# A triangle update and a gated pair layer: reordering the opening of the first stage

## The chip, the cores and the metric

The kernel runs on one core of a Trainium2 chip. The metric is the device time of one execution in microseconds; the time given for a kernel is the median of several executions. One further execution is taken with the hardware profiler, and the profile and the trace in this text come from it.

## The reference, cut to what matters

The input x is a 384 x 384 x 128 array in float32. Two layers follow each other. All matrices are 128 x 128.

```python
def _L0_conv_ref(z, ...):
    z_n = _layernorm(z, norm_g, norm_b)
    a = _linear(z_n, Wa, ba) * sigmoid(_linear(z_n, Wga, bga))
    b = _linear(z_n, Wb, bb) * sigmoid(_linear(z_n, Wgb, bgb))
    x = einsum('bijd,bjkd->bikd', a, b)
    x = _layernorm(x, normo_g, normo_b)
    return z + _linear(x, Wo, bo) * sigmoid(_linear(z_n, Wgo, bgo))

def _L1_conv_ref(pair, ...):
    left = pair @ W_left + b_left + (pair @ W_eq + b_eq)
    right_sum = sum(pair @ W_right + b_right, axis=2, keepdims=True)
    gate = sigmoid(pair @ W_gate + b_gate)
    out = (left * right_sum * gate) @ W_out + b_out
    return _layer_norm(out + pair, ln_scale, ln_bias)
```

Layer 0 needs, for every pixel, five products of the normalised x: the two factors a and b with their gates, and the output gate.

## The kernel before, in words

There are three stages. Stage 1 computes a, b and the output gate and writes them to arrays A, B and G in device memory, together with Z, which is x plus a bias. Stage 2 forms the 128 products over j, one for each channel, and the sums for the second norm. Stage 3 does the output product, the gate and all of layer 1. The change concerns only the beginning of stage 1.

Stage 1 works on tiles of x of 128 rows by 16 columns by 128 channels (1 MB). There are 72 tiles, each is done in four steps (TS) of four columns (CT), so there are 288 steps, numbered s; n is the tile and t the quarter. The schedule is manual: each engine executes its instructions in the order in which the program text emits them. An instruction that waits therefore holds up everything behind it on its engine or queue. The engines are PE (TensorE, the products), DVE (VectorE), ACT (ScalarE), POOL (GpSimd) and SP (SyncE, which issues most transfers).

One column of x goes through these helpers:

- `statistics` (DVE): bn_stats and bn_aggr give its mean and variance.
- `norm_factors` (POOL): four small operations make the reciprocal deviation `rstd` (with a power operation) and the offset `off`, for four to sixteen columns at a time.
- `normalise` (ACT): one instruction for each column writes the normalised column `zn`.
- `turn` (PE) transposes four columns into PSUM (`ptr`), and `turned_out` (ACT) copies them to SBUF as `zT`.
- `step` then forms, on PE in this order, `pga`, `pa`, `pgb`, the transposes of the next step, `pb`, and four small products `pgo`. ACT takes the sigmoids `sga` and `sgb`; DVE multiplies into `at` and `bt` and adds the gate's bias into `gs`. The sigmoid of `gs` (`gate`) is taken by ACT during the next step.
- `residual` (POOL): x plus b_out for a whole tile (`zb`), and the transfer to Z that follows it. POOL's queue also issues the transfers to A (after the tile's last `at`) and to G (after its last `gate`).

All products of stage 1 and the weights' preparation take their PSUM from one pool of six buffers (`pk`), which are used in turn: a product can start when the buffer six places earlier has been read. Four buffers hold x tiles, so the fetch of tile n+3 (at the first step of tile n) waits until tile n-1 has been read by all, its residual included.

Before step 0, `prepare` turns each weight: PE transposes it, DVE copies it (`raw`) and scales it by the norm's vector (`scaled`), and PE multiplies it with the norm's bias to give a correction of the weight's bias, which DVE adds. The transfers on SP stand in the order: four quarters of x's first tile, the norm's two vectors, the four biases, x's second tile, and so on. ACT's queue issues the five weights. `prepare` of ga and of a stand ahead of all statistics on DVE.

In the first four steps, DVE computes the statistics of four columns of tile 1 and of four columns of tile 2 in each step; from step 4 on, of four columns two tiles ahead. After step 4 the output weights are prepared: `ob_w`, `prepare("o")`, `center` (the identity less 1/128), the product `pc` of the two, and the sums and scalings of the weights and biases for layer 1. The residuals of tiles 0, 1 and 2 are computed in steps 4, 5 and 6, those of tile 3 and later each at the second step of the tile before.

Of the kernel before, what the change touches and what calls it, by code (L numbers as in the profile page):

```python
# [8 lines left out]
FP = mybir.dt.float32  # L9
AF = mybir.ActivationFunctionType  # L10
ALU = mybir.AluOpType
# [8 lines left out]
def kernel(ctx: ExitStack, tc: tile.TileContext, ins, out: bass.AP):  # L20
# [15 lines left out]
    nc = tc.nc  # L36
    ctx.enter_context(tc.manual_schedule())
    P = 128
    x = ins["x"][0]
    N, C = x.shape[1], x.shape[2]  # L40
# [46 lines left out]

    CG, CX, CT, BR = 64, 16, 4, 32  # L90
    TS = CX // CT
    NT = NB * (N // CX)
    with tc.tile_pool(name="wprep", bufs=6) as wp, tc.tile_pool(name="p1x", bufs=4) as px, tc.tile_pool(name="p1s", bufs=3) as ps, tc.tile_pool(
# [7 lines left out]
            rb, c = divmod(n, N // CX)  # L101
            return rb * P, c * CX

        def fetch(n, parts=1):
            if n >= NT:
                return
            r0, c0 = place(n)
            xt = px.tile([P, CX, C], FP, tag="xt", name=f"xt_{n}")
            for k in range(0, CX, CX // parts):
                nc.sync.dma_start(  # L110
                    out=xt[:, k : k + CX // parts, :], in_=x[r0 : r0 + P, c0 + k : c0 + k + CX // parts, :]
                )
            tiles[n] = {
                "x": xt,
                "st": ps.tile([P, CX, 6], FP, tag="st", name=f"st_{n}"),
                "mv": ps.tile([P, CX, 2], FP, tag="mv", name=f"mv_{n}"),
                "rstd": ps.tile([P, CX], FP, tag="rstd", name=f"rstd_{n}"),
                "off": ps.tile([P, CX], FP, tag="off", name=f"off_{n}"),
            }

        def statistics(n, t):
            if n >= NT:
                return
            for c in range(t * CT, (t + 1) * CT):
                nc.vector.bn_stats(tiles[n]["st"][:, c, :], tiles[n]["x"][:, c, :])  # L125
                nc.vector.bn_aggr(tiles[n]["mv"][:, c, :], tiles[n]["st"][:, c, :])

# [11 lines left out]
        def normalise(n, t, cs=range(CT)):  # L139
            if n >= NT:  # L140
                return
            g = tiles[n]
            for c in (t * CT + k for k in cs):
                nc.scalar.activation(  # L144
                    g["zn"][:, c, :], g["x"][:, c, :], AF.Identity,
                    bias=g["off"][:, c : c + 1], scale=g["rstd"][:, c : c + 1],
                )
# [25 lines left out]
        def gate(s):  # L173
# [4 lines left out]
            if t == TS - 1:  # L178
                r0, c0 = place(n)
                nc.gpsimd.dma_start(out=G[r0 : r0 + P, c0 : c0 + CX, :], in_=gt)  # L180
                tiles.pop(n - 1, None)

        def step(s):
            n, t = divmod(s, TS)
            r0, c0 = place(n)
            if t == 0:
                fetch(n + 3)
                if n:
                    norm_factors(n + 1)
                tiles[n]["at"] = po.tile([P, CX, P], FP, tag="at", name=f"at_{n}")  # L190
                tiles[n]["gt"] = po.tile([P, CX, C], FP, tag="gt", name=f"gt_{n}")
                if c0 % CG == 0:
                    bts[n // (CG // CX)] = po.tile([P, P, CG], FP, tag="bt", name=f"bt_{n}")
            at, bt = tiles[n]["at"], bts[n // (CG // CX)]
            k0 = c0 % CG + t * CT
            zT = turned.pop(s)
            ahead = (n + 1, t - 1) if t else (n, TS - 1)

            def proj(k):
                pk = ppp.tile([P, CT, P], FP, tag="pk", name=f"p{k}_{s}")  # L200
                nc.tensor.matmul(pk, lhsT=wT[k], rhs=zT, start=True, stop=True)  # L201
                return pk

            def sigmoid(k, pg):
                sg = ps.tile([P, CT, P], FP, tag="sg", name=f"sg{k}_{s}")
                nc.scalar.activation(sg, pg, AF.Sigmoid, bias=bcol["g" + k])  # L206
                return sg

            if n == 0:
                statistics(1, t)  # L210
                norm_factors(1, t * CT, t * CT + CT)
            statistics(n + 2, t)
            pga, pa = proj("ga"), proj("a")
            sga = sigmoid("a", pga)
            if s:
                gate(s - 1)
            normalise(*ahead, range(CT // 2))
            nc.vector.scalar_tensor_tensor(  # L218
                at[:, t * CT : (t + 1) * CT, :], pa, bcol["a"], sga, ALU.add, ALU.mult
            )  # L220
            if t == TS - 1:
                nc.gpsimd.dma_start(out=A[:, c0 : c0 + CX, r0 : r0 + P], in_=at)  # L222
            pgb = proj("gb")
            sgb = sigmoid("b", pgb)
            turn(s + 1)
            turned_out(s + 1)
            normalise(*ahead, range(CT // 2, CT))
            pb = proj("b")
            nc.vector.scalar_tensor_tensor(  # L229
                bt[:, :, k0 : k0 + CT].rearrange("d r c -> d c r"), pb, bcol["b"], sgb, ALU.add, ALU.mult  # L230
            )
            pgo = ppp.tile([P, CT, C], FP, tag="pk", name=f"pgo_{s}")
            for c in range(CT):
                nc.tensor.matmul(pgo[:, c, :], lhsT=zT[:, c, :], rhs=wT["go"], start=True, stop=True)  # L234
            gs = ps.tile([P, CT, C], FP, tag="gs", name=f"gs_{s}")
            nc.vector.tensor_tensor(gs, pgo, over(gate_bias, CT), ALU.add)
            gated[s] = gs
            if n == 1 and t < 3:
                residual(t)
            if n > 1 and t == 1:  # L240
                residual(n + 1)
            if k0 + CT == CG:
                b_out_of.extend((bt, r0, c0 + CX - CG, k) for k in range(0, P, BR))
            if t == TS - 1:
                store_b(len(b_out_of) if n == NT - 1 else 1)
# [11 lines left out]
        def prepare(k):  # L257
            both = ppp.tile([P, CT, P], FP, tag="pk", name="w_" + k)
            pt, pb = both[:, 0, :], both[:, 1, :]
            nc.tensor.transpose(pt, wT[k], ident)  # L260
            raw = wp.tile([P, P], FP, tag="raw", name="raw_" + k, bufs=2)
            nc.vector.tensor_copy(raw, pt)
            scaled = ctile([P, P], "wT_" + k)
            nc.vector.tensor_scalar(scaled, raw, og if k == "o" else ng, None, ALU.mult)
            if k in ("go", "o"):
                bias = o_bias if k == "o" else gate_bias
                nc.tensor.matmul(pb, lhsT=ob_w if k == "o" else nb_w, rhs=raw, start=True, stop=True)
                nc.vector.tensor_tensor(bias, pb, bias, ALU.add)
            else:
                nc.tensor.matmul(pb[:, 0:1], lhsT=raw, rhs=nb, start=True, stop=True)  # L270
                nc.vector.tensor_tensor(bcol[k], pb[:, 0:1], bcol[k], ALU.add)
            wT[k] = scaled

        fetch(0, TS)
        for k in ("ga", "a", "gb", "b", "go"):
            weight(k, nc.scalar)
        ng, nb = column(L0 + "norm_g"), column(L0 + "norm_b")
        for k in ("ga", "a", "gb", "b"):
            bcol[k] = column(L0 + "b" + k)
        fetch(1)  # L280
        gate_bias = rows(L0 + "bgo")
        fetch(2)
        b_out, b_off = rows(L1 + "b_out"), column(L1 + "b_out")
        og, ob, o_bias = column(L0 + "normo_g"), column(L0 + "normo_b"), rows(L0 + "bo")
# [4 lines left out]
        b_left, b_eq, b_right, b_gate = (column(L1 + k) for k in ("b_left", "b_eq", "b_right", "b_gate"))  # L289
        ln_s, ln_b = rows(L1 + "ln_scale"), rows(L1 + "ln_bias")  # L290

        prepare("ga")
        prepare("a")
        for t in range(TS):
            statistics(0, t)
            norm_factors(0, t * CT, t * CT + CT)
            if t < TS - 1:
                normalise(0, t)
            if t == 0:
                turn(0)  # L300
                turned_out(0)
                prepare("gb")
                prepare("b")
                nc.vector.tensor_copy(nb_w, nb.to_broadcast([P, P]))
            if t == 1:
                prepare("go")
        for s in range(NT * TS):
            step(s)
            if s == TS:
                nc.vector.tensor_copy(ob_w, ob.to_broadcast([P, P]))  # L310
                prepare("o")
                nc.vector.tensor_scalar(center, ident, -1.0 / C, None, ALU.add)
                pc = ppp.tile([P, CT, P], FP, tag="pk", name="pc")[:, 0, :]
                nc.tensor.matmul(pc, lhsT=center, rhs=wT["o"], start=True, stop=True)
                nc.vector.tensor_copy(w_o0, pc)
                nc.vector.tensor_copy(w_o0[0:1, :], o_bias[0:1, :])
                nc.vector.tensor_tensor(w_left, w_left, w_eq, ALU.add)
                nc.vector.tensor_tensor(b_left, b_left, b_eq, ALU.add)
                nc.vector.tensor_scalar(b_right, b_right, float(N), None, ALU.mult)
                nc.vector.tensor_scalar(b_off, b_off, -1.0, None, ALU.mult)  # L320
        gate(NT * TS - 1)


# [304 lines left out]
```

## Time and profile before

| | |
|---|---|
| median of 3 executions | 3382.05 us (3381.01 to 3382.28) |
| the profiled execution | 3381.63 us |
| its span, first to last instruction | 3379.9 us |
| mean granted TensorE clock | 0.99 |
| PE busy | 3293.1 us (97% of the span) |
| DVE busy | 2668.5 us (79%) |
| ACT busy | 2308.5 us (68%) |
| POOL busy | 2088.7 us (62%) |
| moved | 910.52 MB, mean 269 GB/s |

All times of single instructions below count from the start of the span. Busy time is the time in which an engine executes; instructions of one engine can overlap a little at their ends. In a timeline row the columns are the start, the duration of the group, the engine, the line of the kernel, the operation with what it writes and reads, the shapes and the number of instructions; in brackets stands how long the engine had been idle and what released it. PE's busy time is that of the matrix products alone, and the loading of weights (PEld) runs beside it.

### The profile page before, as it was taken

To read this page: it belongs to the slowest core of one execution; us is meant where nothing else is said; L and a number is where in the kernel's file an instruction comes from. 1 tells how busy PE (TensorE), PEld (TensorE's weight loads), DVE (VectorE), ACT (ScalarE), POOL (GpSimd) and SP (SyncE) were. 2 spreads that over 40 slices of the span, in tenths; PEclk is the share of its full clock that TensorE was granted. 3 is DMA by queue.
4 is the path that set the end of the run, shared out by engine and by line. 5 is a ranking of instruction groups with operands and counts; after the bars stand their busy time and mean duration, and the time that the engine had idled before them with its cause. 6 is when DMAs were issued, how large, how long until landed. Compare 5 with 4: busy or idle time off the path is not lost.

```text
span 3379.9 us, 53338 instructions
## 1 busy us (share of the span) xinstructions
PE 3293.1 (97%) x15581; PEld 2194.0 (65%) x15581; DVE 2668.5 (79%) x8599; ACT 2308.5 (68%) x5488; POOL 2088.7 (62%) x1562
## 2 busy tenths in 40 slices
PE   7999999999999999699999999999999999999997
PEld 4555555555555555355555555578888888888885
DVE  7777777777777777445555555699999999999998
ACT  5777877877787778422222222378888888888887
POOL 5555555555555555345555555448888888888887
PEclk9999999999999999899999999999999999999998
DMA  5888899999998899799999999867777777777773
GB/s 179 261 276 268 259 275 283 276 285 278 279 281 274 254 275 281 213 344 304 304 308 305 303 308 307 273 220 264 264 264 263 265 264 263 263 264 262 263 262 141
DMA packets 675330, 910.52 MB, mean 269 GB/s; under 512 B 319328, under 2 KB 616288, under 8 KB 647520
## 3 DMA queue, kind: packets, MB, share of 16 engines
q1 hardware_dynamic: 634000, 680.28, 63.7%
q0 software_dynamic: 40320, 226.51, 19.4%
q8 instruction: 126, 2.06, 0.2%
q14 instruction: 164, 1.34, 0.1%
q10 hardware_dynamic: 720, 0.33, 0.0%
HBM read 454.04 MB, written 452.98 MB: 268 GB/s over the span
## 4 chain that ended last, share of the span: by engine, by line
PE 84%; DVE 12%; DMA 1%; POOL 1%; SPq 1%; issue 0%; ACT 0%; ACTq 0%; POOLq 0%; DVEq 0%
PE pm L410 22%; PE pgo L234 8%; PE pga L201 7%; PE pa L201 7%; PE pgb L201 7%; PE pb L201 7%; PE pleft L546 5%; PE py L505 5%; PE pf L495 5%; PE pg L548 5%; PE ptr L163 4%; DVE py L511 3%; PE ptr L469 2%; DVE st L516 2%; DVE h L483 2%; DVE res L496 2%
## 5 line engine op out<-in xcount | busy, mean ns | idle before, releaser
L410 PE MATMUL pm<-bd,ad 128*128 128x384 f32 x2304 | 746.1, 487 | 31.4 <-DMA bd<-B 31.4
L410 PEld LDWEIGHTS pm<-bd,ad 128*128 128x128 f32 x2304 | 439.3, 191 | 337.3 <-issue 34.0
L425 POOL TENSOR_TENSOR s<-s,xd 128x384 f32<-128x384 f32 x381 | 379.7, 997 | 396.2 <-DVE xd L418 396.1
L423 ACT ACTIVATE sq<-xd 128x384 f32<-128x384 f32 x381 | 188.5, 495 | 544.9 <-DVE xd L418 544.9
L229 DVE SCALAR_TENSOR_TENSOR bt<-pb,c_L_conv_bb,sgb 128x512 f32<-128x512 f32 x288 | 321.0, 1115 | 246.1 <-ACT zT L170 240.1
L144 ACT ACTIVATE zn<-xt,off,rstd 128x128 f32<-128x128 f32 x1152 | 504.5, 489 | 15.5 <-POOL off L135 15.5
L418 DVE TENSOR_TENSOR xd<-pm,x 128x384 f32<-128x384 f32 x381 | 212.2, 557 | 376.8 <-POOL s L425 321.4
L538 ACT ACTIVATE res<-res,off,rs 128x128 f32<-128x128 f32 x1152 | 482.5, 486 | 26.8 <-POOL off L532 24.4
L222 POOL DMA_DIRECT2D A<-at x72 | 85.3, 1184 | 552.6 <-DVE at L218 552.6
L206 ACT ACTIVATE sga<-pga,c_L_conv_bga 128x512 f32<-128x512 f32 x288 | 197.9, 687 | 287.1 <-PE pga L201 287.1
L234 PEld LDWEIGHTS pgo<-wT_go,zT 128*128 128x128 f32 x2304 | 302.6, 192 | 137.6 <-issue 72.4
L511 DVE SCALAR_TENSOR_TENSOR py<-py,rs,gr 128x128 f32<-128x128 f32 x1152 | 384.0, 333 | 1.7 <-PE py L505 1.0
L154 POOL TENSOR_TENSOR zb<-xt,r_L_conv_b_out 128x2048 f32<-128x2048 f32 x72 | 328.0, 4556 | 4.3 <-DMA Z<-zb 2.5
L578 POOL TENSOR_TENSOR res<-res,r_L_conv_ln_bias 128x1536 f32<-128x1536 f32 x94 | 324.6, 3453 | 7.4
L495 PE MATMUL pf<-w_o,h 128*128 128x128 f32 x2304 | 321.3, 276 | 6.1 <-ACT w_o L477 5.3
L577 POOL TENSOR_TENSOR res<-res,r_L_conv_ln_scale 128x1536 f32<-128x1536 f32 x94 | 325.3, 3461 | 0.1
L505 PE MATMUL py<-w_o,xr 128*128 128x128 f32 x2304 | 320.9, 276 | 0.9 <-DVE xd L418 0.9
L546 PE MATMUL pleft<-pairT,m_L_conv_W_left 128*128 128x384 f32 x768 | 313.1, 489 | 3.1 <-ACT pairT L471 3.1
L553 ACT ACTIVATE sg<-pg,c_L_conv_b_gate 128x384 f32<-128x384 f32 x384 | 222.8, 580 | 136.4 <-PE pg L548 84.7
L516 DVE BATCH_NORM_STATS2 st<-res 128x6 f32<-128x128 f32 x1152 | 312.2, 272 | 0.3
L548 PE MATMUL pg<-pairT,m_L_conv_W_gate 128*128 128x384 f32 x768 | 311.2, 487 | 0.0
L125 DVE BATCH_NORM_STATS2 st<-xt 128x6 f32<-128x128 f32 x1152 | 305.7, 265 | 0.2 <-issue 0.2
(131 smaller groups left out, 6753.5 us busy)
## 6 DMA issues: line engine op xcount, KB each, us to landing
A<-at POOLq DMA_DIRECT2D x72, 1024.0 KB, 7.4
G<-gt POOLq DMA_DIRECT2D x72, 1024.0 KB, 8.5
Z<-zb POOLq DMA_DIRECT2D x72, 1024.0 KB, 8.1
B<-bt SPq DMA_DIRECT2D x72, 1024.0 KB, 16.7
ad<-A SPq DMA_DIRECT2D x128, 576.0 KB, 6.9
bd<-B SPq DMA_DIRECT2D x128, 576.0 KB, 8.0
xr<-X SPq DMA_DIRECT2D x96, 768.0 KB, 6.0
gr<-G SPq DMA_DIRECT2D x96, 768.0 KB, 7.6
```

Source lines behind the costliest of these rows:

```text
L144: nc.scalar.activation(g["zn"][:, c, :], g["x"][:, c, :], AF.Identity, bias=g["off"][:, c : c + 1], scale=g["rstd"][:, c : c + 1],)
L201: nc.tensor.matmul(pk, lhsT=wT[k], rhs=zT, start=True, stop=True)
L234: nc.tensor.matmul(pgo[:, c, :], lhsT=zT[:, c, :], rhs=wT["go"], start=True, stop=True)
L410: nc.tensor.matmul(pm, lhsT=ad[:, q, ib * P : (ib + 1) * P], rhs=bd[:, q, :], start=(q == 0), stop=(q == NB - 1),)
L425: nc.gpsimd.tensor_tensor(s1[:, ib, :], s1[:, ib, :], xd, ALU.add)
L495: nc.tensor.matmul(pf[:, q, :], lhsT=h[:, q * P : (q + 1) * P], rhs=w_o, start=True, stop=True)
L505: nc.tensor.matmul(py[:, q, :], lhsT=g["x"][:, i, q * P : (q + 1) * P], rhs=w_o0, start=True, stop=True)
L511: nc.vector.scalar_tensor_tensor(py[:, q, :], py[:, q, :], rs0[:, q, u : u + 1], g["g"][:, i, q, :], ALU.mult, ALU.mult)
L516: nc.vector.bn_stats(b["st"][:, k, q, :], b["res"][:, k, q, :])
L538: nc.scalar.activation(g["res"][:, i, q, :], g["res"][:, i, q, :], AF.Identity, bias=g["off"][:, i, q : q + 1], scale=g["rs"][:, i, q : q ...
L546: nc.tensor.matmul(pleft, lhsT=w_left, rhs=pairT, start=True, stop=True)
L548: nc.tensor.matmul(pg[:, 0:N], lhsT=w_gate, rhs=pairT, start=True, stop=True)
```

## The change

The change orders the opening of stage 1 anew. No arithmetic of the result is changed except in how the output weights are put together.

- Transfers: SP issues only the first quarter of x's first tile, then the norm's two vectors and two biases, the second quarter, two more biases, the third and fourth quarters, the gate's bias, and then the second tile.
- ACT takes one sigmoid of 16 dummy columns (`warm`) directly after issuing the weights.
- The statistics and factors of the first quarter, and its normalise, stand ahead of `prepare` of ga and a; those of the second quarter follow `turn(0)`, those of the third and fourth stand around `prepare("go")`. The third and fourth quarter are normalised in step 0, after the copy of `zT`.
- `statistics` counts columns through all tiles. In steps 0 to 3 it does four columns a step (tile 1), in steps 4 to 11 six, and from step 12 (CATCH_UP) four again, by then two tiles ahead as before. The factors of tiles 1 to 3 come in pieces by a table.
- Up to step 11 all four normalises of a step stand behind the copy of `zT`; later, two stand ahead of it and two behind, as before.
- The residuals of tiles 0 to 3 move to steps 3, 6, 8 and 10.
- The output weights are prepared in three pieces after steps 12, 13 and 14 instead of in one after step 4, and w_o is scaled straight from PSUM.

```diff
-        def statistics(n, t):
-            if n >= NT:
-                return
-            for c in range(t * CT, (t + 1) * CT):
+        def statistics(first, last):
+            for k in range(first, min(last, NT * CX)):
+                n, c = divmod(k, CX)
...
+        CATCH_UP = 3 * TS
+        FIRST_FACTORS = {
+            0: ((1, 0, 4),), 1: ((1, 4, 8),), 2: ((1, 8, 12),), 3: ((1, 12, 16),),
+            4: ((2, 0, 4),), 5: ((2, 4, 12),), 6: ((2, 12, 16),), 7: ((3, 0, 8),), 9: ((3, 8, 16),),
+        }
+        FIRST_RESIDUALS = {3: 0, 6: 1, 8: 2, 10: 3}
+
+        def columns_ahead(s):
+            return CX + CT * s + 2 * min(max(s - TS, 0), 2 * TS)
...
-                if n:
+                if s >= CATCH_UP:
                     norm_factors(n + 1)
...
-            if n == 0:
-                statistics(1, t)
-                norm_factors(1, t * CT, t * CT + CT)
-            statistics(n + 2, t)
+            statistics(columns_ahead(s), columns_ahead(s + 1))
+            for factors in FIRST_FACTORS.get(s, ()):
+                norm_factors(*factors)
...
-            normalise(*ahead, range(CT // 2))
+            if s >= CATCH_UP:
+                normalise(*ahead, range(CT // 2))
...
-            normalise(*ahead, range(CT // 2, CT))
+            if s == 0:
+                normalise(0, 2)
+            normalise(*ahead, range(CT // 2 if s >= CATCH_UP else 0, CT))
...
-            if n == 1 and t < 3:
-                residual(t)
-            if n > 1 and t == 1:
+            if s < CATCH_UP:
+                if s in FIRST_RESIDUALS:
+                    residual(FIRST_RESIDUALS[s])
+            elif t == 1:
                 residual(n + 1)
...
+        def last_weights():
+
+            nc.vector.tensor_copy(ob_w, ob.to_broadcast([P, P]))
+            nc.vector.tensor_scalar(center, ident, -1.0 / C, None, ALU.add)
+            pt = ppp.tile([P, CT, P], FP, tag="pk", name="pt_o")[:, 0, :]
+            nc.tensor.transpose(pt, wT["o"], ident)
+            raw, scaled = (wp.tile([P, P], FP, tag="raw", name=k + "_o", bufs=2) for k in ("raw", "scaled"))
+            nc.vector.tensor_copy(raw, pt)
+            nc.vector.tensor_scalar(scaled, pt, og, None, ALU.mult)
+            yield
+            nc.vector.tensor_tensor(w_left, w_left, w_eq, ALU.add)
+            nc.vector.tensor_tensor(b_left, b_left, b_eq, ALU.add)
+            yield
+            both = ppp.tile([P, CT, P], FP, tag="pk", name="both_o")
+            nc.tensor.matmul(both[:, 0, :], lhsT=center, rhs=scaled, start=True, stop=True)
+            nc.tensor.matmul(both[:, 1, :], lhsT=ob_w, rhs=raw, start=True, stop=True)
+            nc.vector.tensor_scalar(b_right, b_right, float(N), None, ALU.mult)
+            nc.vector.tensor_scalar(b_off, b_off, -1.0, None, ALU.mult)
+            nc.vector.tensor_copy(w_o0, both[:, 0, :])
+            nc.vector.tensor_tensor(o_bias, both[:, 1, :], o_bias, ALU.add)
+            nc.vector.tensor_copy(w_o0[0:1, :], o_bias[0:1, :])
+
+        warm = wp.tile([P, 16], FP, tag="warm", name="warm", bufs=1)
+        x_parts = fetch_parts(0, TS)
+        next(x_parts)
         for k in ("ga", "a", "gb", "b", "go"):
             weight(k, nc.scalar)
+        nc.scalar.activation(warm, mhalf, AF.Sigmoid)
         ng, nb = column(L0 + "norm_g"), column(L0 + "norm_b")
         for k in ("ga", "a", "gb", "b"):
             bcol[k] = column(L0 + "b" + k)
+            if k in ("a", "b"):
+                next(x_parts)
+        for _ in x_parts:
+            pass
+        gate_bias = rows(L0 + "bgo")
         fetch(1)
-        gate_bias = rows(L0 + "bgo")
...
+        first_quarter(0)
+        normalise(0, 0)
         prepare("ga")
         prepare("a")
-        for t in range(TS):
-            statistics(0, t)
-            norm_factors(0, t * CT, t * CT + CT)
...
+        turn(0)
+        turned_out(0)
+        first_quarter(1)
+        normalise(0, 1)
+        prepare("gb")
+        prepare("b")
+        first_quarter(2)
+        nc.vector.tensor_copy(nb_w, nb.to_broadcast([P, P]))
+        prepare("go")
+        first_quarter(3)
+        later = last_weights()
         for s in range(NT * TS):
             step(s)
-            if s == TS:
-                nc.vector.tensor_copy(ob_w, ob.to_broadcast([P, P]))
-                prepare("o")
-                nc.vector.tensor_scalar(center, ident, -1.0 / C, None, ALU.add)
...
+            if s >= CATCH_UP:
+                next(later, None)
```

(`first_quarter(t)` is `statistics` and then `norm_factors` for quarter t of tile 0. `fetch_parts` is the old `fetch` as a generator that stops after each transfer.)

More of the change, by code (lines that the diff above doesn't have):

```diff
@@ L102, in place, with fetch, fetch_parts @@
             return rb * P, c * CX
-        def fetch(n, parts=1):
+        def fetch(n):
+            for _ in fetch_parts(n, 1):
+                pass
+        def fetch_parts(n, parts):
             if n >= NT:
@@ L108, in fetch @@
             xt = px.tile([P, CX, C], FP, tag="xt", name=f"xt_{n}")
[L109 to L112, printed above, removed]
             tiles[n] = {
@@ L119, in fetch @@
             }
-        def statistics(n, t):
-            if n >= NT:
-                return
-            for c in range(t * CT, (t + 1) * CT):
+            for k in range(0, CX, CX // parts):
+                nc.sync.dma_start(
+                    out=xt[:, k : k + CX // parts, :], in_=x[r0 : r0 + P, c0 + k : c0 + k + CX // parts, :]
+                )
+                yield
+        def statistics(first, last):
+            for k in range(first, min(last, NT * CX)):
+                n, c = divmod(k, CX)
                 nc.vector.bn_stats(tiles[n]["st"][:, c, :], tiles[n]["x"][:, c, :])
@@ L263, in prepare @@
             scaled = ctile([P, P], "wT_" + k)
[L264 to L268, printed above, removed]
+            nc.vector.tensor_scalar(scaled, raw, ng, None, ALU.mult)
+            if k == "go":
+                nc.tensor.matmul(pb, lhsT=nb_w, rhs=raw, start=True, stop=True)
+                nc.vector.tensor_tensor(gate_bias, pb, gate_bias, ALU.add)
             else:
@@ L272, in prepare @@
             wT[k] = scaled
-        fetch(0, TS)
+        def last_weights():
[9 more added lines that the diff above has]
+            nc.vector.tensor_tensor(b_left, b_left, b_eq, ALU.add)
+            yield
+            both = ppp.tile([P, CT, P], FP, tag="pk", name="both_o")
[9 more added lines that the diff above has]
+        next(x_parts)
         for k in ("ga", "a", "gb", "b", "go"):
             weight(k, nc.scalar)
+        nc.scalar.activation(warm, mhalf, AF.Sigmoid)
         ng, nb = column(L0 + "norm_g"), column(L0 + "norm_b")
@@ L279 @@
             bcol[k] = column(L0 + "b" + k)
+            if k in ("a", "b"):
+                next(x_parts)
+        for _ in x_parts:
+            pass
+        gate_bias = rows(L0 + "bgo")
         fetch(1)
-        gate_bias = rows(L0 + "bgo")
         fetch(2)
@@ L290, with first_quarter @@
         ln_s, ln_b = rows(L1 + "ln_scale"), rows(L1 + "ln_bias")
+        def first_quarter(t):
+            statistics(t * CT, t * CT + CT)
+            norm_factors(0, t * CT, t * CT + CT)
+        first_quarter(0)
+        normalise(0, 0)
         prepare("ga")
         prepare("a")
-        for t in range(TS):
-            statistics(0, t)
-            norm_factors(0, t * CT, t * CT + CT)
[L297 to L306, printed above, removed]
+        turn(0)
[9 more added lines that the diff above has]
+        later = last_weights()
         for s in range(NT * TS):
             step(s)
-            if s == TS:
-                nc.vector.tensor_copy(ob_w, ob.to_broadcast([P, P]))
-                prepare("o")
[L312 to L320, printed above, removed]
+            if s >= CATCH_UP:
+                next(later, None)
         gate(NT * TS - 1)
```

## The prediction

> **What bounds the kernel now.** First the page's summary and its row of 40 slices: PE is 97% busy, and a slice is 84.5 us.
>
> ```profile
> PE   7999999999999999699999999999999999999997
> ```
>
> Only the first slice, the one with the change from stage 1 to stage 2, and the last stay below 9. So PE sets the end, and a change confined to the opening can only fill holes that PE has there. Second, the stretches view, cut at the starts of pga (the first product of a step) of steps 0, 1, 4, 5, 6, 8 and 16. Its columns are the stretch, its length, the busy time of each engine, the granted TensorE clock, the DMA share and GB/s.
>
> ```profile
> 0.00:21.07 21.07, 6.14 (x19) 3.93 (x20) 6.46 (x31) 3.52 (x6) 3.12 (x13) 1.00 0.63 193
> 21.07:30.79 9.72, 7.46 (x22) 3.60 (x21) 7.31 (x35) 7.13 (x15) 6.17 (x15) 1.00 0.41 122
> 30.79:45.19 14.40, 14.40 (x61) 8.51 (x61) 13.63 (x53) 11.53 (x25) 4.21 (x10) 1.00 0.01 2
> 45.19:58.08 12.89, 6.14 (x27) 3.77 (x26) 11.63 (x22) 4.59 (x10) 11.57 (x11) 0.82 0.48 163
> 58.08:65.64 7.56, 7.56 (x21) 3.88 (x21) 7.14 (x16) 3.91 (x8) 5.17 (x3) 0.63 1.02 296
> 65.64:75.17 9.53, 9.53 (x42) 5.61 (x41) 7.88 (x23) 7.50 (x16) 6.33 (x3) 1.00 0.77 316
> 75.17:113.30 38.13, 38.13 (x163) 22.44 (x161) 29.98 (x89) 30.36 (x65) 21.23 (x16) 1.00 0.56 194
> ```
>
> From 75.17 on, eight steps take 38.13, so a step is 4.766 us of PE without a hole; the same view gives PE 1224.83 busy of 1224.83 us from 75.17 to 1300. Whatever step 8 gains is therefore carried to the end of stage 1, and the 31.4 us that PE idles there follow the last B stores, which move along. The opening's cost is all in front of 75.17: 21.07 us until step 0, then an excess over 4.766 of 4.95 (step 0), 8.12 (step 4) and 2.79 (step 5).
>
> Third, the timeline of the opening: why step 0 is late and long.
>
> ```profile
> 4.06 1.28 ACT L144 ACT_TABLE_LOAD   x1 [4.06 <-DMA xt<-in_x_dram]
> 7.75 0.29 DVE L264 TENSOR_SCALAR wT_ga<-raw_ga,c_L_conv_norm_g 128x128 f32<-128x128 f32 x1 [2.66 <-DMA c_L_conv_norm_g<-in_L_conv_norm_g_dram]
> 9.90 0.28 DVE L125 BATCH_NORM_STATS2 st<-xt 128x6 f32<-128x128 f32 x1
> 13.68 1.65 ACT L144 ACTIVATE zn<-xt,off,rstd 128x128 f32<-128x128 f32 x4 [8.33 <-POOL off L135]
> 20.48 0.79 PE L267 MATMUL w_go<-raw_go,nb_w 128*128 128x128 f32 x2 [1.85 <-DVE raw_go L262]
> 21.07 1.91 PE L201 MATMUL pga<-zT,wT_ga 128*128 128x512 f32 x2
> 26.94 1.28 ACT L206 ACT_TABLE_LOAD   x1
> 28.24 0.69 ACT L206 ACTIVATE sga<-pga,c_L_conv_bga 128x512 f32<-128x512 f32 x1
> ```
>
> x's first quarter is there at 4.06, but DVE stands at the first weight until the norm's vector lands at 7.75, and its statistics start at 9.90. The first sigmoid waits behind twelve normalises and a table load to 28.24, with its product complete at 22.98. pga takes 1.91 here against 1.02 warm: PE runs at half speed until about 26.2.
>
> Fourth, the stall between steps 4 and 5.
>
> ```profile
> 52.78 4.51 POOL L154 TENSOR_TENSOR zb<-xt,r_L_conv_b_out 128x2048 f32<-128x2048 f32 x1
> ...
> 52.91 4.47 DVE L312 TENSOR_SCALAR center<-ident 128x128 f32<-128x128 f32 x1
> 57.53 0.77 PE L314 MATMUL pc<-wT_o,center 128*128 128x128 f32 x2 [4.86 <-DVE center L312]
> 58.17 4.52 POOL L154 TENSOR_TENSOR zb<-xt,r_L_conv_b_out 128x2048 f32<-128x2048 f32 x1
> 58.66 4.13 DVE L316 COPY w_o<-r_L_conv_bo 1x128 f32<-1x128 f32 x1
> ```
>
> Two small DVE operations, whose like take 0.2 to 0.3, last until 0.1 us after the end of POOL's residual beside them; PE waits for the first one in program order, then starts again at half speed.
>
> **The change part by part**, on the profiled execution's clock.
>
> *Statistics first.* They start at 4.06. Every following length is one of before: four columns 1.68 (9.90 to 11.58), POOL's factors 2.06 (to 13.64), normalise to the last transpose's start 1.74 (13.64 to 15.38). DVE does ga and a in POOL's shadow, 5.75 to 8.0. The two vectors now stand second and third on SP, at about 1.7 and 2.1 (a quarter takes 0.95 to issue), and with 3.1 us to landing they are there by 5.3, before their use at 6.1. Then the second quarter's statistics 8.0 to 9.7; gb and b 2.9 us after the last transpose's start at 9.54 (15.64 to 18.52 before), so to 12.7; third quarter to 14.35; nb_w 0.22; raw_go 14.5, its bias product 14.9, and pga of step 0 at 15.4 (0.59 later, as before). Gain 5.7. The quarters pushed back on SP issue by 7.3 at the latest and need 3.5, against needs at 8.0, 12.7 and 14.9: nothing. The sigmoid table's load moves to 3.1 to 4.4, when ACT waits for its first normalise at 7.8: nothing, and 1.28 if that cover were gone.
>
> *Step 0.* Its sigmoid waits for nothing but pga now, and DVE has 4 statistics columns in the step instead of 8. PE runs through: 5.1 cold (pga, pa, pgb as before, 21.07 to 26.18), ptr 0.43, pb 0.86, pgo 0.89, together 7.29 instead of 9.72: gain 2.4. pga of step 1 is at 22.7. Eight normalises, 3.3 us, are moved into ACT's step 0 behind the copy of zT; the next copy ends at 27.4, when PE is free at 27.46: I charge 0.1.
>
> *Steps 1 to 11.* DVE per step: a column 0.395, at 0.65, bt 0.94, gs 0.60. With 8 columns (steps 0 to 3 before) 5.35, and the trace shows 5.36 there: DVE was the bound, covered by buffers. With 4 it is 3.77, with 6 (steps 4 to 11 now) 4.56, below 4.766. ACT: 0.57+0.52+0.57+0.47+1.67 = 3.8. POOL is where the margin is thin. residual(0), moved from step 4 to step 3, is 4.55 plus 0.57 for Z's issue, and the first factors of tile 2 queue behind it: ready 3.6 after pga of step 5, needed at 4.0. All later factor sets have 2.8 us or more. x's tile 4 can be fetched when residual(0) has read tile 0, at 42.8, lands by 50, and is first read in step 9 at 61. So no hole, and I charge nothing; the cover is DVE's spare 0.2 us a step, and without it (six columns at their busy 0.46) DVE would need 4.95 and cost 0.2 a step, 1.5 us over eight. Step 4's 8.12 and step 5's 2.79 go. pga of step 8 stands at 22.7+0.1+7*4.766 = 56.2 instead of 75.17: 19.0 us earlier.
>
> *Output weights after steps 12 to 14.* Here something comes back. In the like step of before (pga at 94.23):
>
> ```profile
> 94.23 1.02 PE L201 MATMUL pga<-zT,wT_ga 128*128 128x512 f32 x2
> ...
> 99.06 4.55 POOL L154 TENSOR_TENSOR zb<-xt,r_L_conv_b_out 128x2048 f32<-128x2048 f32 x1
> ...
> 99.34 0.69 DVE L236 TENSOR_TENSOR gs<-pgo,r_L_conv_bgo 128x512 f32<-128x512 f32 x1
> ```
>
> POOL's residual starts 4.83 after pga, DVE is free for ob_w and center at 5.71. Two more columns in step 11 delay at, hence A's issue, the factors and this residual, by 0.7: about 5.5, still 0.2 ahead of DVE. By the row, center then waits to 10.1. Behind it queue raw and scaled (to 11.1), step 13's statistics (12.7), at (13.35), bt, gs (14.9). The copies of w_o's transpose free the sixth PSUM buffer, which pga of step 14 wants at 9.65: it starts at 11.1. gate(13) waits for gs, and behind it on ACT stand 2 normalises, sgb and zT of step 15: 17.5 instead of 14.3. Loss 3.1 with PE's own small products in it. PE is never idle over 1.5 us, so I charge no cold start. The last pieces meet no residual (that of tile 5 comes 19 us later): 1 us of DVE, within its slack.
>
> [...] By row and my 0.2 us, 3.1. I take 3.1. [...]
>
> [...] The row gives 5.1 us of cold work; [...] I keep the row.
>
> Sum: 5.7+2.4-0.1+8.1+2.8 = 18.9 (19.0 unrounded), less 3.1: 15.9. The profiled execution's 3381.63 becomes 3365.7; it lies 0.4 below the median, so 3366.2 for the median.
>
> **The rivals.** (1) DVE passes the residual at step 12: 18.2 gained, 3363.9. For it: a margin of 0.2 us. Against: POOL would have to be 0.5 later. 0.20. (2) The catch-up is less smooth: late factors of tile 2, a late x quarter or a wait of DVE at each residual give holes of 4 to 8 us, 3370 to 3374. For it: the 0.4 us margin at step 5. 0.12. (3) Slower: the factor sets queue behind residuals 0 to 3 on POOL, and ACT stands at each. If a residual's whole 5.1 us comes through four times, 20.5 us are lost: 3386.7. It decides from 4 us per place. Against: the margins worked out above are 0.4 once and then 2.8 and more. 0.04. (4) It doesn't do what it says: step 0 stays bound by something that the timeline hides (a vector landing late), and the stall only moves: 3376 to 3382. 0.04. My forecast has 0.60.
>
> **How the numbers follow.** The forecast's own range, [...] is 3364 to 3369. The range takes in rival 1 at its early end and rival 2 in part: 3361.5 to 3372. About 0.2%, 6.8 us, is what a measurement of this kernel can tell from no change: faster beyond that 0.91, within it 0.05, slower 0.04.
>
> **What would show it.** pga of step 0 near 15.4, of step 1 near 22.7, of step 8 near 56; one table load before the first sigmoid; no PE hole of over 1 us from step 1 to 13; center of about 4.5 us beside residual 4 and a hole of some 3 us around steps 14 and 15. Wrong if pga of step 8 comes after 60, if ACT waits for POOL's off in steps 5 to 11, or if the rest of stage 1 does not keep 4.766 a step.

## The result, and the profile after

The changed kernel takes 3363.74 us (median of 6 runs, 3362.64 to 3364.85) against 3381.81 us before (6 runs): a ratio of 0.9948, 95% interval 0.9937 to 0.9958. 18.1 us are gained, where 15.9 were forecast; the time lies just under the forecast's own range of 3364 to 3369. The profiled execution took 3363.57 us, its span is 3361.8.

In the summary of the changed kernel, PE is 98% busy. In its row of slices only the first differs from before, an 8 in place of the 7:

```profile
PE   8999999999999999699999999999999999999997
```

The stretches view, cut at pga of steps 0, 1, 8, 12, 16 and 24 (stretch, its length, busy time of each engine, clock, DMA share, GB/s):

```profile
0.00:14.82 14.82, 6.17 (x19) 3.94 (x20) 7.93 (x39) 5.38 (x11) 4.99 (x17) 1.00 0.70 211
14.82:21.25 6.43, 6.43 (x21) 3.39 (x21) 4.50 (x19) 2.67 (x6) 4.43 (x11) 1.00 0.50 148
21.25:54.61 33.36, 33.36 (x142) 19.63 (x141) 29.19 (x94) 28.62 (x61) 22.64 (x30) 1.00 0.50 162
54.61:73.68 19.07, 19.07 (x83) 11.22 (x82) 17.89 (x61) 15.65 (x34) 17.80 (x16) 1.00 0.95 327
73.68:95.53 21.85, 20.11 (x87) 11.91 (x86) 20.39 (x56) 15.98 (x35) 10.24 (x9) 1.00 0.53 196
95.53:133.66 38.13, 38.13 (x163) 22.43 (x161) 30.17 (x89) 30.39 (x65) 22.39 (x17) 1.00 0.96 291
```

Step 0 starts at 14.82 instead of 21.07 and takes 6.43 instead of 9.72. Then PE is busy for the whole of eleven steps: 33.36 and 19.07 are 7 and 4 times 4.766. Step 8 comes at 54.61 instead of 75.17, 20.6 earlier. From step 0 on, the stretch from step 12 to step 16 is the only one with a hole: 21.85 instead of 19.06, 2.8 us given back. After it, eight steps take 38.13, to the hundredth as before. 20.6 less 2.8 is 17.8; the spans differ by 18.1, so the later stages carry the gain and add 0.3.

The timeline of the changed kernel, opening (chosen rows):

```profile
3.63 0.29 DVE L130 BATCH_NORM_STATS2 st<-xt 128x6 f32<-128x128 f32 x1 [3.63 <-DMA xt<-in_x_dram]
7.43 1.65 ACT L149 ACTIVATE zn<-xt,off,rstd 128x128 f32<-128x128 f32 x4 [1.75 <-POOL off L140]
14.23 0.80 PE L285 MATMUL w_go<-raw_go,nb_w 128*128 128x128 f32 x2 [1.84 <-DVE raw_go L281]
14.82 1.92 PE L217 MATMUL pga<-zT,wT_ga 128*128 128x512 f32 x2
16.77 0.69 ACT L222 ACTIVATE sga<-pga,c_L_conv_bga 128x512 f32<-128x512 f32 x1 [3.81 <-PE pga L217]
18.20 1.02 PE L217 MATMUL pgb<-zT,wT_gb 128*128 128x512 f32 x2
```

The statistics wait for x alone, and the first sigmoid waits for its own product alone (it started 5.3 us after its product was complete before, and 0.03 us now). The last row is a warm product (1.02 us): PE has this speed from 18.20 on, 3.38 us after the start of step 0. Before, it took 5.11 (21.07 to 26.18). The clock column of the stretches view reads 1.00 in step 0 all the same; that PE is slower there is read from the lengths. pga takes 1.92 here, as it does in step 5 of the kernel before, where the column falls to 0.63 (from 58.08 to 62.00 it reads 0.50).

The timeline around the output weights (chosen rows):

```profile
79.12 4.53 POOL L159 TENSOR_TENSOR zb<-xt,r_L_conv_b_out 128x2048 f32<-128x2048 f32 x1
79.38 4.37 DVE L294 COPY ob_w<-c_L_conv_normo_b 128x128 f32<-128x128 f32 x1
83.67 0.21 DVE L295 TENSOR_SCALAR center<-ident 128x128 f32<-128x128 f32 x1
84.49 1.10 PE L217 MATMUL pga<-zT,wT_ga 128*128 128x512 f32 x2 [1.01 <-DVE scaled_o L300]
88.17 0.63 ACT L182 ACTIVATE gt<-gs 128x512 f32<-128x512 f32 x1 [1.86 <-DVE gs L254]
90.67 1.12 PE L217 MATMUL pga<-zT,wT_ga 128*128 128x512 f32 x2 [0.73 <-ACT zT L175]
```

The residual of tile 4 starts 0.26 us ahead of ob_w, and ob_w lasts until 0.1 us after the residual's end. The forecast had center waiting; it was ob_w, which stands ahead of it, and center took 0.21. The rest of the chain is there as forecast: PE waits for the PSUM buffer that scaled_o frees, ACT's gate waits for gs, and PE waits for zT behind that gate.

### The profile page after: what moved, and what is told of

The parts are those of the page before. It is cut to its first block, busy times and chain, and to the rows that moved or that the text cites. A ratio compares the mean times of both kernels' runs of the same rounds, so it can differ in the third digit from the quotient of the medians.

```text
span 3361.8 us, 53349 instructions
## 1 busy us (share of the span) xinstructions
PE 3288.6 (98%) x15581; PEld 2191.5 (65%) x15581; DVE 2665.4 (79%) x8599; ACT 2310.0 (69%) x5488; POOL 2093.2 (62%) x1574
## 4 chain that ended last, share of the span: by engine, by line
PE 92%; DVE 5%; DMA 1%; POOL 1%; SPq 0%; ACT 0%; issue 0%; POOLq 0%; ACTq 0%; DVEq 0%
PE pm L451 22%; PE pgo L252 8%; PE pga L217 7%; PE pa L217 7%; PE pb L217 7%; PE pgb L217 7%; PE py L546 7%; PE pf L536 7%; PE pleft L587 7%; PE pg L589 6%; PE ptr L168 4%; PE ptr L510 3%; DVE py L552 1%; DVE st L557 1%; DVE h L524 1%; DVE res L537 1%
## 5 line engine op out<-in xcount | busy, mean ns | idle before, releaser
L552 DVE SCALAR_TENSOR_TENSOR py<-py,rs,gr 128x128 f32<-128x128 f32 x1152 | 436.6, 379 | 1.6 <-PE py L546 1.0
L557 DVE BATCH_NORM_STATS2 st<-res 128x6 f32<-128x128 f32 x1152 | 364.4, 317 | 0.3
```

Of the source, the lines that this page charges most:

```text
L552: nc.vector.scalar_tensor_tensor(py[:, q, :], py[:, q, :], rs0[:, q, u : u + 1], g["g"][:, i, q, :], ALU.mult, ALU.mult)
L557: nc.vector.bn_stats(b["st"][:, k, q, :], b["res"][:, k, q, :])
```

## The experiments

Times are medians of their runs; the kernel before, run beside them, took 3381.54 us in the first four and 3381.7 us in the others. Each kernel's code line numbers are its own. The intervals of the ratios reach some 0.1% (about 4 us) to either side, so differences of 1 to 2 us between the variants are read from the lengths of stretches in the traces; the medians alone do not settle them.

**e1: the output weights one step later.**

```diff
-            if s >= CATCH_UP:
+            if s > CATCH_UP:
                 next(later, None)
```

> The changed kernel with the three pieces of the output weights one step later, after steps 13, 14 and 15. Theory (the loss of 2.8 us at steps 12 to 15 is VectorE waiting for the residual of tile 4, which ends 10.0 us after pga of step 12): after step 13 VectorE comes 10.5 us after that pga, the residual is over, ob_w and center take 0.2 us each, and of the loss only PE's own 0.55 us and at most 0.3 of delay stay: 2.0 us less than the changed kernel, about 3361.7. Rival (the loss is the work itself, the seven small operations and two more PSUM buffers): it only moves, the time stays at 3363.7.

Measured: 3361.67 us, ratio 0.9942 (0.993 to 0.9955). From step 12 to step 17 its trace has 24.38 us, five steps and 0.55. The timeline of e1:

```profile
79.81 4.54 POOL L159 TENSOR_TENSOR zb<-xt,r_L_conv_b_out 128x2048 f32<-128x2048 f32 x1
...
84.86 0.20 DVE L294 COPY ob_w<-c_L_conv_normo_b 128x128 f32<-128x128 f32 x1
84.99 0.26 DVE L295 TENSOR_SCALAR center<-ident 128x128 f32<-128x128 f32 x1
```

The same work, 0.5 us after the residual instead of inside it, takes 0.2 us each. The loss was the wait: the trace loses 0.55 us there instead of 2.79, and the median is 2.1 us lower. The rival, that the work itself costs the time, falls.

**e2: without the dummy sigmoid.**

```diff
-        nc.scalar.activation(warm, mhalf, AF.Sigmoid)
```

> The changed kernel without the dummy sigmoid. Theory: the table load then stands in front of the first sigmoid of step 0, but ScalarE is idle there from 12.97 (end of the second normalise) to 16.77 (pga of step 0), so 1.28 us of load are hidden: 0.0 us, 3363.7. Rival (the early load is a part of the gain in step 0): 1.3 us more, 3365.0.

Measured: 3364.15 us, ratio 0.9948 (0.9936 to 0.996). That is 0.4 from the changed kernel, inside the spread of either. The timeline of e2 shows the load in ACT's hole:

```profile
13.21 1.28 ACT L222 ACT_TABLE_LOAD   x1
17.02 0.69 ACT L222 ACTIVATE sga<-pga,c_L_conv_bga 128x512 f32<-128x512 f32 x1 [2.52 <-PE pga L217]
```

ACT still waits 2.52 us for PE after the load. Once the order of the opening is the new one, the early load has no effect on PE that these runs can tell. What shortened step 0 is shown by e4.

**e3: the output weights alone moved, on the kernel before.** `last_weights` of the change, called after steps 12, 13 and 14; everything else as before.

```diff
-            if s == TS:
-                nc.vector.tensor_copy(ob_w, ob.to_broadcast([P, P]))
-                prepare("o")
...
+            if s >= 3 * TS:
+                next(later, None)
```

> The kernel before with only the output weights moved, in the three pieces after steps 12, 13 and 14. Theory: the 8.1 us at step 4 and the 2.8 us at half clock in step 5 go, and steps 12 to 15 lose some 2.1 us (there VectorE reaches ob_w 0.9 us after the start of the residual of tile 4, so 3.6 us of wait instead of 4.3): 8.8 us less than before, about 3373.0. Rival (the stall at step 4 is a wait for something else beside it, a late transfer or the residual's own queue, and reappears in the next steps): under 5 us.

Measured: 3380.88 us, ratio 0.9998 (0.9989 to 1.0006): 0.7 us, where I expected 8.8. The stall at steps 4 and 5 is gone (5.31 us from pga to pga, then 4.87, which is 10.3 less), but 6.9 come back at steps 9 and 10 (9.10 and 7.33), and 2.2 at steps 12 to 15, as I had expected there. The timeline of e3:

```profile
66.05 4.55 POOL L154 TENSOR_TENSOR zb<-xt,r_L_conv_b_out 128x2048 f32<-128x2048 f32 x1 [2.46 <-DMA Z<-zb]
70.90 0.57 POOL L155 DMA_DIRECT2D Z<-zb  x1 [0.30 <-POOL zb L154]
71.47 1.19 POOL L222 DMA_DIRECT2D A<-at  x1
...
73.08 2.94 POOL L133 TENSOR_TENSOR rstd<-rstd,mhalf 128x16 f32<-128x16 f32 x1
...
76.72 0.88 ACT L144 ACTIVATE zn<-xt,off,rstd 128x128 f32<-128x128 f32 x2 [4.86 <-POOL off L135]
78.70 2.07 PE L201 MATMUL pga<-zT,wT_ga 128*128 128x512 f32 x2 [4.17 <-ACT zT L170]
```

Three residuals stand in a row on POOL, the third waits for a buffer of Z, and the factors of tile 3 queue behind it. ACT stands 4.86 us for `off`, PE 4.17 for zT, and then PE starts cold (2.07 against 1.02). In the kernel before, the stall at step 4 had hidden this. There the factors of tile 3 were ready at 79.18, and step 9 began at 79.94; here they are ready at 76.69, but step 9 begins at 69.60. My expectation had looked at one stall and not asked what is late next; the rival's figure, under 5 us, was the right one.

**e4: the order up to step 0 alone, on the kernel before.** The change's transfers, dummy sigmoid and `first_quarter` order; statistics of the steps, residuals and output weights as before.

```diff
+        first_quarter(0)
+        normalise(0, 0)
         prepare("ga")
         prepare("a")
-        for t in range(TS):
-            statistics(0, t)
...
+        first_quarter(2)
+        normalise(0, 2)
```

> The kernel before with only the new order up to step 0: the transfers, the dummy sigmoid, statistics and factors of a quarter ahead of the weights (the third quarter is still normalised before step 0). Statistics of the first steps, residuals and output weights are as before. Theory: pga of step 0 at 14.8 instead of 21.07, pga of step 1 at 21.3 instead of 30.79, then the old stall at step 4: 9.5 us less than before, about 3372.3; with e3 it adds up to the whole change. Rival (VectorE's eight columns in each of steps 0 to 3 were what made step 0 long): pga of step 1 stays later, at 24 or more, and only 6 us are gained.

Measured: 3371.71 us, ratio 0.9972 (0.9961 to 0.9982), 9.8 us less. The stretches view of e4, cut at pga of steps 0, 1, 4, 5 and 6:

```profile
0.00:15.06 15.06, 6.18 (x20) 3.95 (x20) 7.93 (x39) 5.40 (x11) 4.99 (x17) 1.00 0.70 206
15.06:21.25 6.19, 6.08 (x22) 3.22 (x21) 5.53 (x27) 4.21 (x10) 4.41 (x11) 1.00 0.56 157
21.25:35.74 14.49, 14.49 (x60) 8.48 (x60) 13.72 (x53) 11.65 (x25) 4.20 (x11) 1.00 0.28 83
35.74:48.68 12.94, 6.19 (x27) 3.83 (x26) 11.66 (x23) 4.66 (x10) 11.63 (x11) 0.85 0.47 162
48.68:54.84 6.16, 6.16 (x21) 3.37 (x21) 5.78 (x12) 3.90 (x8) 5.18 (x3) 0.77 0.97 287
```

Step 1 starts at 21.25 although DVE does eight columns in step 0; so the columns did not make step 0 long. ACT's rows of e4:

```profile
16.27 1.66 ACT L149 ACTIVATE zn<-xt,off,rstd 128x128 f32<-128x128 f32 x4 [3.07 <-POOL off L140]
17.84 0.67 ACT L211 ACTIVATE sga<-pga,c_L_conv_bga 128x512 f32<-128x512 f32 x1
```

Twelve normalises still stand ahead of the first sigmoid here. But the last four, which wait for POOL's factors, end at 17.9 instead of 26.9, and the sigmoid starts 0.9 us after its product is complete instead of 5.3. So it is the earlier statistics and factors that free step 0, not a smaller number of normalises. (What the table load would cost in this order, without the dummy sigmoid, was not tried.) The old stall at step 4 is whole (12.94 us). With e3 it does *not* add up: 9.8 and 0.7 are 10.5, and the change brings 18.1.

**e5: e3, with the residual of tile 2 behind the factors of tile 3.**

```diff
-            if n == 1 and t < 3:
+            if n == 1 and t < 2:
                 residual(t)
+            if n == 2 and t == 0:
+                residual(2)
```

> e3 (the kernel before with the output weights moved) with one more edit: the residual of tile 2 at step 8 instead of step 6, behind the factors of tile 3 on GpSimd. Theory (in e3 the 6.9 us lost at steps 9 and 10 are the factors of tile 3 queued behind three residuals in a row): ScalarE's wait for off goes, and the time is 7.5 us below before, about 3374.0. Rival (the loss in e3 is bound to the earlier work of VectorE or to x's transfers): it stays within 1.5 us of e3, 3379.5 or more.

Measured: 3374.08 us, ratio 0.9977 (0.9968 to 0.9986), 7.6 us less than before and 6.8 less than e3. In its trace the power operation of tile 3 starts at 66.07 instead of 73.08 and no step from 2 to 11 takes over 4.83 us. (Step 1 takes 6.56 in this profile: PE had idled 3.05 us ahead of it, and its pga, pa and pgb take 1.51, 1.91 and 1.53 against 1.02 warm.) 9.8 (e4) and 7.6 make 17.4 of the 18.1. So, on this kernel, moving the output weights pays only together with a place for the residuals, or the factors, that keeps POOL ahead.

**e6: eight statistics columns in each of the first four steps.**

```diff
-            return CX + CT * s + 2 * min(max(s - TS, 0), 2 * TS)
+            return CX + CT * s + CT * min(s, TS)
```

> The changed kernel with eight statistics columns in each of steps 0 to 3 and four from step 4 on, as before the change. Theory: VectorE then needs 5.35 us in these four steps against 4.77 of PE, and is 2.3 us late after them; 0.7 of that are covered by the gate's slack on ScalarE and 0.7 by the slack of zT, so PE loses about 0.4, at most 1: 3364.1. Rival (the spreading of the statistics is a main part of the gain of step 0): 2.3 us or more, 3366.

Measured: 3362.31 us, ratio 0.9943 (0.993 to 0.9955): 1.4 us *less* than the changed kernel. From step 1 to step 8 it takes 33.48 us, 0.12 more than the changed kernel, so the eight columns cost next to nothing. The gain is at step 12. Timeline of e6:

```profile
80.43 0.22 DVE L294 COPY ob_w<-c_L_conv_normo_b 128x128 f32<-128x128 f32 x1
80.56 0.25 DVE L295 TENSOR_SCALAR center<-ident 128x128 f32<-128x128 f32 x1
...
81.71 4.55 POOL L159 TENSOR_TENSOR zb<-xt,r_L_conv_b_out 128x2048 f32<-128x2048 f32 x1
...
85.32 1.10 DVE L302 TENSOR_TENSOR m_L_conv_W_left<-m_L_conv_W_left,m_L_conv_W_eq 128x128 f32<-128x128 f32 x1
```

Here POOL is behind (its transfer to A starts 1.12 us after pga of step 12 and not 0.39 before it), the residual comes 7.0 us after pga, and ob_w and center are through before it. This is rival 1 of the prediction: DVE passes the residual. The sum of w_left, with two SBUF inputs, now falls into the residual and takes 1.10 instead of 0.28, to 0.16 after its end. The stretch from step 12 to 16 takes 19.62 us, 0.56 more than four steps, and PE is busy for all of it. Rival 1's gain, 18.2 of the 19.0, was an estimate that put 0.8 on this case.

**e7: the residuals of tiles 0 to 3 at their old steps.**

```diff
-        FIRST_RESIDUALS = {3: 0, 6: 1, 8: 2, 10: 3}
+        FIRST_RESIDUALS = {4: 0, 5: 1, 6: 2, 9: 3}
```

> The changed kernel with the residuals of tiles 0 to 3 at steps 4, 5, 6 and 9, as before the change, its factors still in pieces. Theory: by the rows of the changed kernel GpSimd has the last factors of tile 2 at 56 (needed at 58.6) and the first of tile 3 at 63.9 (needed at 63.4), so at most 0.5 us is lost: 3363.7 to 3364.3. Rival (the residuals' places are what keeps GpSimd ahead, as e3 suggests): ScalarE waits for off in step 9 by 3 us or more and PE loses 3 to 7 us.

Measured: 3361.82 us, ratio 0.9941 (0.9929 to 0.9954): 1.9 us less than the changed kernel. No step between 1 and 11 takes over 4.77 us. The list of waits of e7 (engine, line, releaser: us in total, times, longest), ACT, from 22 to 100 us:

```profile
ACT zn L149 <- POOL off L140: 1.3, 1, 1.3
```

ACT waits once for 1.3 us, and its slack covers it. So with the factors in pieces and the four normalises behind the copy of zT, POOL bears even the old places of the residuals; the rival falls. And POOL is again late enough at step 12 that DVE gets through first (residual at 81.55, ob_w at 80.23): 0.56 lost instead of 2.8.

**e8: e1, and go's weight prepared ahead of the third quarter's statistics.**

```diff
-        first_quarter(2)
         nc.vector.tensor_copy(nb_w, nb.to_broadcast([P, P]))
         prepare("go")
+        first_quarter(2)
```

> The changed kernel with e1's edit (output weights after steps 13 to 15) and the gate's weight go prepared ahead of the third quarter's statistics. Theory: pga of step 0 comes 1.5 us earlier (13.3 to 13.6 instead of 14.8 to 15.1), as it waits for that weight's product and VectorE for 1.65 us of statistics in front of it; of the 1.5 about 1.4 arrive at step 1; with the 2.0 of e1: 3360.2. Rival (step 1 is bound by the statistics and at of step 0, which do not come earlier): no more than e1, 3361.7.

Measured: 3360.22 us, ratio 0.9937 (0.9924 to 0.9949): the fastest version, 21.5 us less than before and 3.5 less than the change. In its timeline the first steps start at

```profile
13.68 1.91 PE L217 MATMUL pga<-zT,wT_ga 128*128 128x512 f32 x2
...
20.15 1.02 PE L217 MATMUL pga<-zT,wT_ga 128*128 128x512 f32 x2
```

against 15.09 and 21.96 in e1. Part of the earlier step 1 is PE's speed in step 0: pgb takes 1.03 here and 1.44 in e1, the step 6.47 and 6.87.

## Why the prediction was right, and what was off

The forecast's mechanism held in the main: an earlier step 0, a shorter step 0, eleven steps without a hole, and a loss at steps 12 to 15 through a residual that starts just ahead of ob_w (5.44 after pga, forecast 5.5; DVE at 5.70, forecast 5.71). The sum was 2.2 us too small, and all its misses point the same way, so no two of them cancelled. The number alone would have misled: 3363.74 is nearer to rival 1's 3363.9 than to the forecast's 3366.2. Only the trace tells them apart, since the residual did come first and cost 2.79 us. The terms, measured:

- *Start of step 0:* 5.7 forecast, 6.25 measured. The transfer of x's first quarter landed at 3.63, not 4.06. I had taken 0.95 us to issue a quarter by dividing the group's 3.79 by four; the changed kernel's single issue took 0.38 and a group of two 0.91, so the 3.79 held more than four issues. (The 2.9 us for gb and b, which the text counts from the last transpose, run from gb's own at 15.64; the sum has it so.)
- *Step 0:* 7.29 forecast, 6.43 measured, the largest miss. I kept 5.1 us of cold work from the row; how far it could vary, and so this part of the forecast's range, no trace had shown. The row was one draw and not a constant: from pga to the transposes takes 5.11 us in it, but 4.90 in e3 and 4.33 in e5, which have the same opening. Against 2.58 warm, twice the excess gives 5.1, 4.6 and 3.5 us of cold work, an estimate from cold products that take nearly twice as long as warm ones (1.91 against 1.02). The seven profiles with the new opening (e4 among them) take 3.72 to 4.87, which is 2.3 to 4.6 of cold work. Step 0 takes 6.17 to 7.06 in these seven, all below the forecast. PE's last 6.85 us ahead of step 0 hold the same work at the same distances in the kernel before and in the changed one. Ahead of these PE idled 4.44 us before and 0.54 after; whether that counts was not tried, and this stays open.
- *Step 0's cause:* the gain is that the sigmoid no longer waits behind late normalises. Earlier statistics are enough for that (e4); what the moving of the third quarter's normalises into step 0 adds is not shown. That DVE has four columns instead of eight, which I named beside it, does nothing for step 1 (e4 and e6).
- *Steps 1 to 11:* no hole; the 0.1 charged for eight normalises was not lost. The thinnest margin was thinner than I worked out: the first factors of tile 2 were ready 4.0 us after pga of step 5, not 3.6, and ACT still shows no wait for them.
- *Steps 12 to 15:* 3.1 forecast, 2.79 measured. Scaled was done 10.7 us after pga of step 12, not 11.1; I had added ob_w, center and raw at full length, while they overlap. No cold start came: after PE's two idle times there, 1.01 and 0.73 us, pga takes 1.10 and 1.12. In the kernel before, at step 1, it takes 1.12 after 2.26 idle.
- *The residual and the small operations of DVE:* where the residual starts first, the DVE operation lasts until 0.1 us after its end: center before (4.47 us), ob_w in the changed kernel (4.37). In e6 and e7 ob_w and center are through before the residual starts (0.22 us for ob_w), so whether a DVE operation that has started would hold the residual back, on which rival 1 leaned, these rows do not show. That the residual did not fall behind DVE in the changed kernel was a matter of 0.26 us; with a margin of 0.2 in the forecast, that it fell on this side was in part luck.
- *wT_gb beside a power operation of POOL:* the forecast charged nothing, and nothing was lost. In the changed kernel wT_gb (10.18 to 10.47) runs inside a power operation (9.63 to 10.67) in 0.29 us. The kernel before had no such row for the opening's weights: there wT_go starts at 20.46, ahead of the power operation at 20.65. Why wT_gb does not wait and ob_w does, these runs do not settle.
- *Rival 3,* the factors behind the residuals, does not happen in the changed kernel, but e3 shows its mechanism with its full price in the kernel before. The edit that my text costed at nothing, the residuals, factors and normalises in their new places, is what lets the removed stall count; e5 gives its worth as 6.8 us on the side of the kernel before. Which of the three does it in the changed kernel is only narrowed: not the residuals' places (e7) and not the columns (e6); factors in pieces and the later normalises were not tried apart.

## What to carry to other kernels

When an early stall is removed, everything behind it arrives earlier at its next queue: look there before counting the gain. In e3 POOL's queue, whose lateness the old stall had hidden, took 6.9 us at steps 9 and 10, and 0.7 of the expected 8.8 were left. In an order written out by hand, place small VectorE work of the kinds that waited here (a copy: 4.37 us against 0.22; the addition of a constant: 4.47 against 0.21; a sum of two SBUF tensors: 1.10 against 0.28) outside an addition on GpSimd as long as the residual (4.5 us); a quarter of a microsecond decided between 0.2 and 4.4 us for one copy. The length of PE's cold work in one profile is a draw, not a constant: 5.11, 4.90 and 4.33 us for the same opening.

## What the runs showed of the hardware that I had not expected

- An addition of two SBUF tensors on VectorE that starts inside GpSimd's residual also lasts until 0.16 (e6) and 0.17 us (e7) after its end: 1.10 us in e6 and 1.15 in e7 against 0.28 outside it. Not all VectorE work does: in e6 the statistics (0.26), at (0.73), bt (1.12) and gs (0.68) run inside the same residual and take 0.26, 0.73, 1.11 and 0.69 after it.
- A row's mean duration can differ between profiles of unchanged code. In stage 3, which no kernel here touches, the product with rs took 333 ns in the profile before, 379 in that of the change and 397 to 400 in e1 to e8, with the spans in line with the runs' times; why is not known. So a difference of 20% in one row's mean is no evidence when the stage's length stands still.
